# Five edits to an image network's kernel: RNN input kept in SBUF with its statistics, a scale and shift by ScalarE, PSUM copies by ScalarE, two sets of convolution banks, and B's diagonals built two quarters at a time

## Chip, cores and metric

The kernel runs on one core of a Trainium2 chip, all in fp32. The metric is the device time of one execution in microseconds (us). Engines are named as the profile names them: PE (TensorE, with PEld for its weight loads), DVE (VectorE), ACT (ScalarE), POOL (GpSimd) and SP (SyncE, which issues the DMAs here). A `q` behind an engine's name is its sequencer.

## The reference

Two layers over an image batch x of shape (4, 64, 64, 128): 4 images, 4096 tokens each, 128 channels.

```python
x = x + L0_conv(ln(x))        # attention, 4 heads of 32, q and k scaled to norm 1 over tokens
t = tokens(x)
t = t + L0_ffn(ln(t))         # an RNN over 4096 tokens
x = x + L1_conv(ln(x))        # projection, 3x3 convolution, selective scan, projection
t = tokens(x)
t = t + L1_ffn(ln(t))         # 64 experts, 8 tokens each
```

The parts that the change touches:

```python
# L0_ffn
Wx = t @ W.T
Wx = (Wx - mean) * rsqrt(var + 1e-5) * gamma + beta     # over all tokens of all images
y[t] = sigmoid(Wx[t] + y[t-1] @ V.T)
# L1_conv, d = 256 inner channels, N = 16 states, K = 4 directions
xin, z = split(x @ in_proj.T)
u = silu(conv3x3_depthwise(xin) + conv_b)
dt, B, C = projections of u, per direction
h = h * exp(dt * A) + (dt * u) * B                      # per token, 256 x 16 states
y = sum over n of h * C;  + D * u;  directions summed
y = (y - mean) * rsqrt(var + 1e-5) * norm_g + norm_b    # over the 256 channels
out = (y * silu(z)) @ out_proj.T
```

## The kernel before

Channels lie on the 128 partitions and tokens along the free axis. A chunk is 512 tokens (CH), 8 to an image (NCH). The stages are functions called one after another: `attention`, `rnn`, `selective_scan` (its inputs, the scans, its outputs) and `experts`. Between them the activations x1, wx, x2, x3 lie in DRAM. Each stage opens its own pools of SBUF and PSUM. Instructions go to each engine's queue in a planned order, and an engine works its queue off in that order.

**Norms (L85 to L148).** Every layer norm over channels runs in groups of four chunks. `centre` takes the mean by a matmul (L115), subtracts it on DVE (L117), squares on ACT (L118), and sums the squares by a matmul (L121). `end` makes the reciprocal root for an image; `scale` spreads it over the partitions by a matmul (L145) and multiplies on DVE (L148). Setting up its constants costs a few DVE copies (L100).

**Attention.** `attention_of_small` makes q, k and v per chunk: three groups of four matmuls, where v's result goes from a single PSUM bank `v_ps` to SBUF by a DVE copy (L243). Then the long attend loop writes x1. After it the block with pools `af_w` and `af_p` makes the RNN's input: per image it loads x1 again (`x_wx`), runs Norms, multiplies by `w_ffn` (L484), copies PSUM to SBUF by ACT (L486) and writes `wx` to DRAM (L487). The image ahead is centred before the present one is scaled. Behind it stands a branch, `tc.If(flag > 0)` (L176 and L177), for inputs on which the quick form of the softmax doesn't hold; it isn't taken with this data, but all engines meet there. `attention_of_any` holds the other path with its own `wx` code.

**RNN.** `rnn` loads `v_ffn` and `bn`, then each image's `wx` into one large SBUF tile `z` (L697), with a `bn_stats` on DVE for each of 32 chunks (L699), then `bn_aggr` (L701) and small operations on one column, which give gamma and beta folded into a scale and a shift. They are applied to z image by image (L710). After that come the sweeps of the recurrence.

**Scan inputs.** Per image: norm, projection to xin and z, then `convolved` (from L898). The convolution of one half (h) of the 256 channels is done in two groups of four chunks, c0 = 0 and 4. A group is 288 small matmuls (32x32 diagonal weights, L913) into the 4 banks of one PSUM tile `conv_ps` with `bufs=1`, then 16 ACT operations with Silu (L923) that empty it. When a half is whole, POOL makes a copy turned by columns (`uc`, L931), and both go to DRAM. The last image has nothing after it in this stage. The PSUM tags are: `conv` 4 banks, `mm` 3 and `norm` 1.

**Scans.** A schedule written out by hand (`tc.manual_schedule`) runs 144 windows of 16 tiles, one tile a turn. In each turn PE fills `db` (dt u B, L1226), DVE copies a carry into it (L1257) and scans (L1264), ACT makes decays (L1202), and POOL multiplies by C (L1288); PE sums the products (L1317). A generator, `project`, makes the next window's inputs in steps spread over the turns. B's diagonals `b_diag` (L1148) are part of it: B of one quarter of a window (128 partitions x 16 states) times a 32x32 identity, read from PSUM `b_ps`, 128x512 results. Four quarters a window are done one at a time in three turns: one in the turn of `turned(0)`, two in that of `turned(1)`, one more in the next. Half of them, swapped across partitions, go to `b_other` by DMA (L1159 and on).

**Scan outputs.** Per image, ahead by one: y from the directions is summed (L1455) and normed in two halves of channels; per chunk a DVE `tensor_scalar` for each half applies norm_g and norm_b (L1481), DVE multiplies by silu(z) loaded as `z_back` (L1485), PE projects (L1488), DVE adds x2 loaded as `x_back` (L1493), and the sum goes to x3 (L1494). `x_back` and `z_back` have two buffers.

Of the kernel before, what the change touches and what calls it, by code (L numbers as in the profile page):

```python
# [26 lines left out]
P = 128  # L27
# [135 lines left out]
@with_exitstack  # L163
def attention(ctx, tc, a, x1, wx):

    nc = tc.nc
    flag = ctx.enter_context(tc.tile_pool(name="at_f", bufs=1)).tile(
        [1, 1], mybir.dt.int32, name="flag"
    )
    with ExitStack() as inner:
        attention_of_small(inner, tc, a, x1, wx, flag)  # L176
    with tc.If(nc.values_load(flag) > 0):  # L177
        attention_of_any(tc, a, x1, wx)


def attention_of_small(ctx, tc, a, x1, wx, flag):

# [10 lines left out]
    eps6 = constant(nc, cst, 1e-6, "eps6")  # L193
    eps5 = constant(nc, cst, 1e-5, "eps5")
    norms = Norms(nc, cst, ident, C)
# [4 lines left out]
    bo = loaded(nc, cst, a["bo"], "bo")  # L200
    w_ffn = loaded(nc, cst, a["w_ffn"], "w_ffn")
    same_head = constant(nc, cst, 0.0, "same_head", (P, P))
# [18 lines left out]
    def prepare(b, ln_b, r, big, work, ps):  # L221
# [6 lines left out]
        for c in range(NCH):  # L228
            ln = ln_b[:, chunk(c)]
            if c % 4 == 0:  # L230
                norms.scale(ps, r, c // 4, [[ln_b[:, chunk(c + g)]] for g in range(4)])
            for n, (t, w) in enumerate(((q, wq), (k, wk))):
                pt = ps.tile([P, CH], F32, tag="qk", name="qk_ps")
                nc.tensor.matmul(pt, w, ln, start=True, stop=True)
                nc.vector.tensor_copy(t[:, chunk(c)], pt)
                square = work.tile([P, CH], F32, tag="ln_s", name="qk_square")
                nc.scalar.activation(
                    square, t[:, chunk(c)], AF.Square, accum_out=sums[:, n, c : c + 1]
                )
            pt = ps.tile([P, 4, P], F32, tag="v", name="v_ps", bufs=1)  # L240
            for j in range(4):
                nc.tensor.matmul(pt[:, j, :], ln[:, tokens(j)], wv, start=True, stop=True)
            nc.vector.tensor_copy(v[:, 4 * c : 4 * c + 4, :], pt)  # L243
        norm = work.tile([P, 4, 2], F32, tag="norm", name="norm")
# [188 lines left out]
    with (  # L433
# [23 lines left out]
        attend(stream(), work, ps)  # L457
    with (
        tc.tile_pool(name="af_w", bufs=3) as work,
        tc.tile_pool(name="af_p", bufs=2, space=PSUM) as ps,  # L460
    ):
        def centred(b):
            ln = work.tile([P, L], F32, tag="ln_o", name="ln_o")
            var = norms.begin(ps, 2)
            for n in range(NCH // 4):
                xs = []
                for c in range(4 * n, 4 * n + 4):
                    x = work.tile([P, CH], F32, tag="x", name="x_wx", bufs=8)
                    nc.sync.dma_start(x, x1[b][:, chunk(c)])
                    xs.append([x])  # L470
                norms.centre(ps, work, var, n, xs, [[ln[:, chunk(4 * n + g)]] for g in range(4)])
            return ln, norms.end(work, var, eps5)

        ahead = centred(0)
        for b in range(B):
            ln_b, r = ahead
            if b + 1 < B:
                ahead = centred(b + 1)
            for c in range(NCH):
                ln = ln_b[:, chunk(c)]  # L480
                if c % 4 == 0:
                    norms.scale(ps, r, c // 4, [[ln_b[:, chunk(c + g)]] for g in range(4)])
                pt = ps.tile([P, CH], F32, tag="wx", name="wx_ps")
                nc.tensor.matmul(pt, w_ffn, ln, start=True, stop=True)  # L484
                t = work.tile([P, CH], F32, tag="wx_o", name="wx_o")
                nc.scalar.copy(t, pt)  # L486
                nc.sync.dma_start(wx[b][:, chunk(c)], t)  # L487


@with_exitstack  # L490
def attention_of_any(ctx, tc, a, x1, wx):

# [10 lines left out]
    eps6 = constant(nc, cst, 1e-6, "eps6")  # L503
    eps5 = constant(nc, cst, 1e-5, "eps5")
    wq = loaded(nc, cst, a["wq_each"], "wq")
# [3 lines left out]
    bo = loaded(nc, cst, a["bo"], "bo")  # L509
    w_ffn = loaded(nc, cst, a["w_ffn"], "w_ffn")  # L510
    NJ = L // P
# [133 lines left out]
    def finish(b, x):  # L645
        nc.sync.dma_start(x1[b], x)
        for c in range(NCH):
            ln = work.tile([P, CH], F32, tag="ln_o", name="ln_o", bufs=1)
            layer_norm(nc, ps, work, mean_of, [x[:, chunk(c)]], [ln], eps5)
            pt = ps.tile([P, CH], F32, tag="mm", name="wx_ps")  # L650
            nc.tensor.matmul(pt, w_ffn, ln, start=True, stop=True)
            t = work.tile([P, CH], F32, tag="wx_o", name="wx_o", bufs=1)
            nc.scalar.copy(t, pt)
            nc.sync.dma_start(wx[b][:, chunk(c)], t)

# [16 lines left out]
@with_exitstack  # L672
def rnn(ctx, tc, a, x1, wx, x2):

# [6 lines left out]
    cst = ctx.enter_context(tc.tile_pool(name="rn_c", bufs=1))  # L681
    work = ctx.enter_context(tc.tile_pool(name="rn_w", bufs=2))

    ident = cst.tile([P, P], F32, name="ident")
# [5 lines left out]

    z = cst.tile([P, B, L], F32, name="z")

    y = cst.tile([P, B, L + 1], F32, name="y")
    nc.vector.memset(y[:, :, 0:1], 0.0)
    stats = cst.tile([P, B * NCH, nc.vector.BN_STATS_DIM], F32, name="stats")
    for b in range(B):
        nc.sync.dma_start(z[:, b, :], wx[b])  # L697
        for c in range(NCH):
            nc.vector.bn_stats(stats[:, b * NCH + c, :], z[:, b, chunk(c)])  # L699
    mv = cst.tile([P, nc.vector.BN_AGGR_DIM], F32, name="mv")  # L700
# [61 lines left out]
    with tc.If(nc.values_load(flag) > 0):  # L762
        one_by_one(tc, ident, vt, z, y, x1, x2)


# [67 lines left out]
def scan_inputs(ctx, tc, a, x2, us, gates):  # L833
# [65 lines left out]
    def convolved(b):  # L899
        for h in range(ND):  # L900
            u = big.tile([P, L], F32, tag="u", name=f"u_{b}", bufs=2)
            image = xins[b][:, h, :].rearrange("p (h w) -> p h w", w=HW)
            for c0 in range(0, NCH, 4):
                pt = ps.tile([P, 4, CH], F32, tag="conv", name="conv_ps", bufs=1)
                for n, (dy, dx) in enumerate(taps):
                    left, right = max(0, -dx), min(HW, HW - dx)
                    for i in range(4):
                        first = (c0 + i) * RPC
                        top, end = max(first, -dy), min(first + RPC, HW - dy)
                        for r in range(4):  # L910
                            rows = slice(32 * r, 32 * r + 32)
                            to = pt[32 * i : 32 * i + 32, r, :].rearrange("p (h w) -> p h w", w=HW)
                            nc.tensor.matmul(  # L913
                                to[:, top - first : end - first, left:right],
                                diag[rows, h, 3 * (dy + 1) + dx + 1, :],
                                image[rows, top + dy : end + dy, left + dx : right + dx],
                                start=n == 0,
                                stop=n == len(taps) - 1,
                            )
                for r in range(4):  # L920
                    for i in range(4):
                        rows = slice(32 * i, 32 * i + 32)
                        nc.scalar.activation(  # L923
                            u[32 * r : 32 * r + 32, chunk(c0 + i)],
                            pt[rows, r, :],
                            AF.Silu,
                            bias=b_conv[rows, h, r : r + 1],
                        )
# [31 lines left out]
def scans(ctx, tc, a, us, ys):  # L960
# [104 lines left out]
    def project(v):  # L1065
# [80 lines left out]

        def diagonal(i):
            nc.vector.tensor_mul(  # L1148
                v.b_diag[:, i],
                b_ps[:, i].rearrange("p (n o) -> p n o", o=1).to_broadcast([P, N, 32]),  # L1150
                ident32.rearrange("p (o t) -> p o t", o=1).to_broadcast([P, N, 32]),
            )
# [8 lines left out]
        pt = turned(0)  # L1161
        diagonal(0)
        yield 1
        nc.scalar.copy(v.dtu[:, 0], pt)
        yield 1
        pt = turned(1)
        diagonal(1)
        diagonal(2)
        yield 1
        nc.scalar.copy(v.dtu[:, 1], pt)  # L1170
        diagonal(3)
        v.b_other = work.tile([P, NS, N, 32], F32, tag="b_other", name="b_other")
# [256 lines left out]
def scan_outputs(ctx, tc, a, x2, ys, gates, x3):  # L1429
# [38 lines left out]
    for b in range(B):  # L1468
# [3 lines left out]
        for c in range(NCH):  # L1472
# [7 lines left out]
            for h in range(ND):  # L1480
                nc.vector.tensor_scalar(  # L1481
                    t[:, h, :], t[:, h, :], norm[:, 0, h : h + 1], norm[:, 1, h : h + 1],
                    ALU.mult, ALU.add,
                )
# [209 lines left out]
def model(tc, a, out):  # L1694
    with tc.tile_pool(name="between", bufs=1, space=DRAM) as pool:
# [5 lines left out]

        x1, wx, x2, x3 = (images(name) for name in ("x1", "wx", "x2", "x3"))
        attention(tc, a, x1, wx)
        rnn(tc, a, x1, wx, x2)
        selective_scan(tc, a, x2, x3)
# [89 lines left out]
```

## Time and profile before

Three executions took 10324.86, 10325.43 and 10332.41 us; the median is 10325.43.

| what | value |
|---|---|
| profiled execution, its own time | 10315.29 us |
| its span in the profile | 10313.4 us |
| busy PE, DVE, ACT, POOL | 90%, 86%, 66%, 54% |
| scan of DVE (L1264), 2304 | 4763.3 us, 2067 ns each |
| products of POOL (L1288), 2304 | 4506.1 us, 1971 ns each |
| B's diagonals (L1148), 576 | median 683 ns each |
| v copies (L243), 32 | median 692 ns each |
| scale and shift (L1481), 64 | median 542 ns each |
| input statistics (L699), 32 | median 677 ns each |

| stage | from, to (us) |
|---|---|
| q, k and v | 0, 222 |
| attend | 235, 2674 |
| RNN input (wx) | 2676.7, 2786.9 |
| its load, statistics and scale | 2791.3, 2831.5 |
| RNN sweeps, scan inputs | to 3656.7 |
| scans | 3663, 9626 |
| scan outputs | 9631, 9926 |
| experts | 9927, 10313 |

Busy shares are means over stages with different limits, so a stage has to be read by itself. A line number in a row is that of the code; a group's row gives its busy time and the mean of one instruction. "idle 3.1 <-DMA z" is time in which the engine had nothing to do until that transfer came.

### The profile page before, as it was taken

What the parts mean: (1) busy time and instruction counts of PE and PEld (TensorE: products, weight loads), DVE (VectorE), ACT (ScalarE), POOL (GpSimd) and SP (SyncE); (2) the same over time, 40 slices, a digit from 0 to 9 for tenths busy, and PEclk for the clock granted to TensorE, in tenths of its full rate; (3) what the DMA queues carried; (4) which work ended last, traced back from release to release, by engine and by line L of the source; (5) the groups of instructions that cost most, each with busy time, mean ns of one, the idle gap of its engine ahead of it and who ended that gap; (6) DMA issues with size and microseconds to landing.
All of it is one profiled execution on the core that took longest, in us unless ns stands there. A gap on an engine that the chain in (4) does not pass through costs nothing.

```text
span 10313.4 us, 244132 instructions
## 1 busy us (share of the span) xinstructions
PE 9300.8 (90%) x103920; PEld 4392.6 (43%) x103920; DVE 8853.2 (86%) x8023; ACT 6815.1 (66%) x9682; POOL 5613.4 (54%) x3513
## 2 busy tenths in 40 slices
PE   7999999999798779999999999999999999999766
PEld 3222222222233345555555555555555555555323
DVE  7999999999684169999999999999999999999864
ACT  3888888888464557777677777767777776777211
POOL 0000000000011169999999999999999999999200
PEclk8999999999899889999999999999999999999987
DMA  4000000000213245566555566655555555566634
GB/s 182 7 7 32 9 32 9 7 9 7 106 49 110 109 126 143 139 154 158 150 140 147 141 150 154 156 139 139 150 154 150 149 146 136 146 154 156 203 128 168
DMA packets 529251, 1173.63 MB, mean 114 GB/s; under 512 B 47955, under 2 KB 436635, under 8 KB 498331
## 3 DMA queue, kind: packets, MB, share of 16 engines
q1 hardware_dynamic: 528154, 1157.87, 40.3%
q8 instruction: 828, 13.57, 0.5%
q14 instruction: 269, 2.20, 0.1%
HBM read 816.74 MB, written 190.00 MB: 98 GB/s over the span
## 4 chain that ended last, share of the span: by engine, by line
DVE 50%; issue 8%; PE 3%; DMA 2%; DVEq 1%; POOL 0%; ACT 0%; SPq 0%; POOLq 0%; ACTq 0%
DVE states L1264 42%; DVE db L1257 3%; DVE b_diag L1148 1%; DVE log L1120 1%; PE db L1226 0%; DVE y L1455 0%; DVEq L1264 0%; DVEq L1257 0%; PE pool_ps L1575 0%; PE y L1317 0%; PE norm_mean_ps L115 0%; PE gate_ps L1545 0%; DMA weights<-in_w 0%; PE norm_var L121 0%; POOL products L1288 0%
## 5 line engine op out<-in xcount | busy, mean ns | idle before, releaser
L1264 DVE TENSOR_TENSOR_SCAN states<-decays,db 128x920 f32<-128x920 f32 x2304 | 4763.3, 2067 | 175.8 <-DVE db L1257 4.9
L1288 POOL TENSOR_TENSOR products<-states,c_ring 128x912 f32<-128x912 f32 x2304 | 4506.1, 1971 | 431.5 <-DVE db L1257 168.0
L1202 ACT ACTIVATE decays<-dt,a_logs 128x456 f32<-128x456 f32 x4608 | 3100.2, 676 | 97.6
L1226 PEld LDWEIGHTS db<-b_diag,dtu_t 32*128 32x128 f32 x18432 | 2229.3, 187 | 1792.3 <-issue 1332.9
L1226 PE MATMUL db<-b_diag,dtu_t 32*128 32x128 f32 x18432 | 2631.1, 281 | 375.4 <-DVE states L1264 313.6
L1226 PE MATMUL db<-b_other,dtu_t 32*128 32x128 f32 x18432 | 2669.8, 284 | 5.5 <-DMA b_other<-b_diag 3.2
L1235 PE MATMUL y<-zeros 32*128 32x128 f32 x17224 | 2490.7, 283 | 5.0 <-issue 5.0
L1317 PE MATMUL y<-products,ident 64*64 64x456 f32 x18432 | 2309.3, 569 | 6.7 <-issue 4.1
L1226 PEld LDWEIGHTS db<-b_other,dtu_t 32*128 32x128 f32 x18432 | 2231.7, 187 | 6.2 <-DMA b_other<-b_diag 3.8
L1235 PEld LDWEIGHTS y<-zeros 32*128 32x128 f32 x17224 | 2080.5, 186 | 5.0 <-issue 4.8
L333 DVE TENSOR_TENSOR total<-total,ring 128x2048 f32<-128x2048 f32 x768 | 1759.3, 2291 | 65.9 <-DVE total L333 2.8
masks.py:197 POOL MEMSET ident<- 128x128 f32 x6 | 1.2, 204 | 3103.5 <-SPq L177 2789.6
L301 ACT ACTIVATE ring<-sa 128x2048 f32<-128x2048 f32 x640 | 1203.9, 1881 | 452.0 <-PE sa L286 452.0
L1275 ACT COPY carry<-states 128x8 f32<-128x8 f32 x576 | 117.7, 204 | 1668.0 <-DVE states L1264 1621.7
L310 PE MATMUL av<-ring,v_at 128*32 128x512 f32 x8192 | 1010.0, 599 | 0.1
L286 PE MATMUL sa<-q_at,k_at 32*128 32x512 f32 x5120 | 731.8, 641 | 60.9 <-ACT ring L301 35.4
L301 ACT ACTIVATE ring<-sb 128x1536 f32<-128x1536 f32 x512 | 741.3, 1448 | 0.0
L1317 PEld LDWEIGHTS y<-products,ident 64*64 64x64 f32 x18432 | 492.2, 131 | 332.0 <-issue 52.7
L286 PE MATMUL sb<-q_at,k_at 32*128 32x512 f32 x3072 | 555.3, 615 | 50.7 <-ACT ring L301 50.7
L310 PEld LDWEIGHTS av<-ring,v_at 128*32 128x32 f32 x8192 | 210.4, 109 | 700.9 <-issue 676.3
L1257 DVE COPY db<-states 128x8 f32<-128x8 f32 x1728 | 303.1, 175 | 195.0 <-PE db L1226 13.4
L286 PEld LDWEIGHTS sa<-q_at,k_at 32*128 32x128 f32 x5120 | 200.4, 183 | 616.4 <-ACT ring L301 309.7
(208 smaller groups left out, 9162.8 us busy)
## 6 DMA issues: line engine op xcount, KB each, us to landing
c_ring<-c_rows SPq DMA_DIRECT2D x576, 912.0 KB, 7.5
b_other<-b_diag SPq DMA_DIRECT2D x288, 512.0 KB, 9.6
u<-u_r SPq DMA_DIRECT2D x72, 456.0 KB, 10.0
y_r<-sum SPq DMA_DIRECT2D x72, 456.0 KB, 4.2
u<-u_c SPq DMA_DIRECT2D x72, 456.0 KB, 10.1
y_c<-sum SPq DMA_DIRECT2D x72, 456.0 KB, 4.6
weights<-in_w SPq DMA_DIRECT2D x32, 1024.0 KB, 11.9
x<-x SPq DMA_DIRECT2D x96, 256.0 KB, 2.7
```

The source lines that it names most:

```text
L286: nc.tensor.matmul(s[:, m, :], k[rows, tokens(t)], q[rows, chunk(chunk_state["c"])], start=True, stop=True,)
L301: nc.scalar.activation(ring[:, lo : lo + n, :], s[:, at : at + n, :], AF.Exp)
L310: nc.tensor.matmul(chunk_state["av"][rows, :], chunk_state["v"][:, t, rows], ring[:, at + i, :], start=t == 0, stop=t == NJ - 1,)
L333: nc.vector.tensor_add(total, total, w)
L1202: nc.scalar.activation(to, dt, AF.Exp, scale=scale)
L1226: nc.tensor.matmul(bank.rearrange("p (n t) -> p n t", n=4)[:, :, at : at + 32], v.dtu[rows, h, s, :], b[rows, s, 4 * self.q : 4 * self.q + ...
L1235: nc.tensor.matmul(y[:, idle // 2, :P], zeros[rows], zeros[rows], start=False, stop=False)
L1257: nc.vector.tensor_copy(self.edge(self.db[:, SKIP:], v.into), self.edge(before.slot(states), v.outof) if self.nth else self.carry(),)
L1264: nc.vector.tensor_tensor_scan(order(self.slot(states)), order(self.slot(decays, 1 if self.v.back else 0)), order(self.db[:, SKIP:][:, : 2 ...
L1275: nc.scalar.copy(self.carry(), self.edge(self.slot(states), self.v.outof))
L1288: nc.gpsimd.tensor_mul(to, h, c)
L1317: nc.tensor.matmul(to, ident[rows, rows], of, start=begins, stop=ends)
```

## The change

There are five edits.

1. `wx` in DRAM is gone. The block that made it leaves `attention_of_small` and becomes `rnn_inputs`, called in `rnn` after the branch. ACT copies each chunk from PSUM straight into `z`, and the chunk's `bn_stats` is issued right behind the copy. Norms are set up once more there, and `w_ffn` is loaded there. The buffers of the centred image go from 3 to 2. `attention_of_any` loses its `wx` code as well. The tile `y` is made after the block.
2. The v copies are made by ACT instead of DVE.
3. In the last image's convolution the groups c0 = 4 use three banks of `mm` and the one of `norm` instead of `conv`.
4. B's diagonals are made two quarters at a time: `diagonals(0)` in the turn of the first, `diagonals(2)` in that of the second and third; nothing is left in the next turn.
5. Scale and shift in the scan's outputs are ACT operations (Identity with a column of scales and one of biases) instead of DVE ones.

```diff
@@ attention_of_small
-            nc.vector.tensor_copy(v[:, 4 * c : 4 * c + 4, :], pt)
+            nc.scalar.copy(v[:, 4 * c : 4 * c + 4, :], pt)
...
-    with (
-        tc.tile_pool(name="af_w", bufs=3) as work,
-        tc.tile_pool(name="af_p", bufs=2, space=PSUM) as ps,
-    ):
...
-                pt = ps.tile([P, CH], F32, tag="wx", name="wx_ps")
-                nc.tensor.matmul(pt, w_ffn, ln, start=True, stop=True)
-                t = work.tile([P, CH], F32, tag="wx_o", name="wx_o")
-                nc.scalar.copy(t, pt)
-                nc.sync.dma_start(wx[b][:, chunk(c)], t)
@@ rnn
     z = cst.tile([P, B, L], F32, name="z")
+    stats = cst.tile([P, B * NCH, nc.vector.BN_STATS_DIM], F32, name="stats")
+    with ExitStack() as inner:
+        rnn_inputs(inner, tc, a, x1, ident, eps5, z, stats)
...
-    for b in range(B):
-        nc.sync.dma_start(z[:, b, :], wx[b])
-        for c in range(NCH):
-            nc.vector.bn_stats(stats[:, b * NCH + c, :], z[:, b, chunk(c)])
@@ new
+def rnn_inputs(ctx, tc, a, x1, ident, eps5, z, stats):
+    nc = tc.nc
+    cst = ctx.enter_context(tc.tile_pool(name="ri_c", bufs=1))
+    work = ctx.enter_context(tc.tile_pool(name="ri_w", bufs=2))
+    ps = ctx.enter_context(tc.tile_pool(name="ri_p", bufs=2, space=PSUM))
+    norms = Norms(nc, cst, ident, C)
+    w_ffn = loaded(nc, cst, a["w_ffn"], "w_ffn")
...
+    ahead = centred(0)
+    for b in range(B):
+        ln, r = ahead
+        if b + 1 < B:
+            ahead = centred(b + 1)
+        for c in range(NCH):
+            if c % 4 == 0:
+                norms.scale(ps, r, c // 4, [[ln[:, chunk(c + g)]] for g in range(4)])
+            pt = ps.tile([P, CH], F32, tag="wx", name="wx_ps")
+            nc.tensor.matmul(pt, w_ffn, ln[:, chunk(c)], start=True, stop=True)
+            nc.scalar.copy(z[:, b, chunk(c)], pt)
+            nc.vector.bn_stats(stats[:, b * NCH + c, :], z[:, b, chunk(c)])
@@ convolved
-                pt = ps.tile([P, 4, CH], F32, tag="conv", name="conv_ps", bufs=1)
+                if b == B - 1 and c0:
+                    pt = [ps.tile([P, CH], F32, tag="mm", name="conv_ps") for _ in range(3)]
+                    pt.append(ps.tile([P, CH], F32, tag="norm", name="conv_ps", bufs=1))
+                else:
+                    pt = ps.tile([P, 4, CH], F32, tag="conv", name="conv_ps", bufs=1)
+                    pt = [pt[:, r, :] for r in range(4)]
@@ project
-        def diagonal(i):
+        def diagonals(i):
             nc.vector.tensor_mul(
-                v.b_diag[:, i],
-                b_ps[:, i].rearrange("p (n o) -> p n o", o=1).to_broadcast([P, N, 32]),
-                ident32.rearrange("p (o t) -> p o t", o=1).to_broadcast([P, N, 32]),
+                v.b_diag[:, i : i + 2].rearrange("p s n t -> p (s n) t"),
+                b_ps[:, i : i + 2]
+                .rearrange("p s (n o) -> p (s n) o", o=1)
+                .to_broadcast([P, 2 * N, 32]),
+                ident32.rearrange("p (o t) -> p o t", o=1).to_broadcast([P, 2 * N, 32]),
             )
...
         pt = turned(0)
-        diagonal(0)
+        diagonals(0)
...
         pt = turned(1)
-        diagonal(1)
-        diagonal(2)
+        diagonals(2)
         yield 1
         nc.scalar.copy(v.dtu[:, 1], pt)
-        diagonal(3)
@@ scan_outputs
             for h in range(ND):
-                nc.vector.tensor_scalar(
-                    t[:, h, :], t[:, h, :], norm[:, 0, h : h + 1], norm[:, 1, h : h + 1],
-                    ALU.mult, ALU.add,
-                )
+                nc.scalar.activation(
+                    t[:, h, :],
+                    t[:, h, :],
+                    AF.Identity,
+                    scale=norm[:, 0, h : h + 1],
+                    bias=norm[:, 1, h : h + 1],
+                )
```

## The prediction

> **What bounds the kernel now.** I read the page's chain of waits first, then the timeline around the convolution, then the one around the RNN's input, then the busy time by stretches, then VectorE (DVE) alone inside the scan. The profiled execution took 10315.29 us (span 10313.4, 1.9 around it), 10.1 less than the median 10325.43; I sum against the execution and carry the sum over to the median.
>
> The chain, by engine and by line:
>
> ```profile
> DVE 50%; issue 8%; PE 3%; DMA 2%; DVEq 1%; POOL 0%; ACT 0%; SPq 0%; POOLq 0%; ACTq 0%
> DVE states L1264 42%; DVE db L1257 3%; DVE b_diag L1148 1%; DVE log L1120 1%; PE db L1226 0%; DVE y L1455 0%; DVEq L1264 0%; DVEq L1257 0%; PE pool_ps L1575 0%; PE y L1317 0%; PE norm_mean_ps L115 0%; PE gate_ps L1545 0%; DMA weights<-in_w 0%; PE norm_var L121 0%; POOL products L1288 0%
> ```
>
> The scan's VectorE work ends last, and B's diagonals (L1148) stand on it. The stages follow one another behind barriers, so a stage that ends earlier moves everything after it. The last image's convolution (columns: start, duration, engine, line, what; in brackets the idle time before):
>
> ```profile
> 3558.00 10.71 PE L913 MATMUL conv_ps<-xin,diag 32*32 32x512 f32 x286
> 3568.79 11.06 ACT L923 ACTIVATE u<-conv_ps,b_conv 32x512 f32<-32x512 f32 x16 [10.09 <-PE conv_ps L913]
> 3579.91 11.56 PE L913 MATMUL conv_ps<-xin,diag 32*32 32x512 f32 x288 [11.20 <-ACT u L923]
> 3591.57 11.06 ACT L923 ACTIVATE u<-conv_ps,b_conv 32x512 f32<-32x512 f32 x16 [11.72 <-PE conv_ps L913]
> ...
> 3638.43 11.06 ACT L923 ACTIVATE u<-conv_ps,b_conv 32x512 f32<-32x512 f32 x16 [12.44 <-PE conv_ps L913]
> ...
> 3649.61 7.06 POOL L931 COPY uc<-u 128x4096 f32<-128x4096 f32 x1 [39.47 <-ACT u L923]
> ```
>
> TensorE and ScalarE take turns, each idle while the other works, and the stage's last copy waits for the eighth turn. The seam between attention and the RNN:
>
> ```profile
> 2786.01 0.59 ACT L486 COPY wx_o<-wx_ps 128x512 f32<-128x512 f32 x1 [0.28 <-PE wx_ps L484]
> ...
> 2791.28 0.34 SPq L159 DMA_DIRECT2D v_ffn<-in_v_ffn  x1
> ...
> 2792.14 2.13 SPq L697 DMA_DIRECT2D z<-wx  x4
> ...
> 2800.28 19.56 DVE L699 BATCH_NORM_STATS2 stats<-z 128x6 f32<-128x512 f32 x32 [6.32 <-DMA z<-wx]
> 2819.87 1.02 DVE L701 BATCH_NORM_AGGREGATE mv<-stats 128x2 f32<-128x192 f32 x1
> ```
>
> After the last copy come a barrier, a load, and 32 statistics alone on the path. Stretches (start:end, length, then busy PE, PEld, DVE, ACT, POOL, granted clock, DMA share):
>
> ```profile
> 2676.00:2791.00 115.00, 100.42 (x256) 30.70 (x256) 54.65 (x71) 42.67 (x69) 0.11 (x1) 0.93 0.42 148
> 9719.00:9784.00 65.00, 50.56 (x112) 16.25 (x112) 59.63 (x82) 10.27 (x17) 0.00 (x0) 0.89 0.76 250
> 9848.00:9926.00 78.00, 52.72 (x84) 18.32 (x84) 60.83 (x93) 0.00 (x0) 0.00 (x0) 0.76 0.60 192
> ```
>
> In the first TensorE is full and VectorE half idle; in the others, from the scan's output stage, VectorE is nearly full.
>
> **RNN input in SBUF.** From the end of the last L486 copy (2786.60) to the aggregate (2819.87) are 33.3 us: all of it goes except a last statistic behind its copy. The 32 statistics (0.677 each, 0.61 apart) move into the 115 us where VectorE is busy 55; they stand in its queue behind ScalarE's copies, and the next image's centring and L148 products queue behind them, and TensorE's next matmuls for those. Laying them by hand between the rows costs under 1 us per image, mostly caught up, 0.4 at the end. The 32 writes of 256 KB (L487) and 4 loads of z leave SP's queue. But the barrier of the branch now stands ahead of this stage: last x1 write issued until 2674.94, plus the 4.34 that the barrier takes at the seam (last wx issue ends 2786.94, first issue after it 2791.28) is 2679.3; three small weight issues (0.34 to 0.45 each) make the first x load 2680.5 instead of 2676.72: 3.8 later. The new Norms constants (VectorE 1.8 us) hide under that load's 5.4. Aggregate at 2786.6+3.8+0.4+1.0 = 2791.8: **−28** (−32 if the barrier is short; −24 if the statistics hold up the products by 1 us an image).
>
> **v copies to ScalarE.** 32 copies of 0.69 leave VectorE, 32 of some 0.59 (L486's form) join ScalarE, which is busy about 2.2 of each chunk's 2.6 us with them. TensorE paces the chunks (three groups of 0.86), so both are hidden; the v bank is released 0.2 to 0.4 us ahead of its next use. VectorE's 13.5 us at image ends no longer hold v: **−1** (−7, if all of TensorE's waits for L243, 4.3 us, and its followers go, to +4 if the slack is short by 0.12 in each of 32 chunks).
>
> **Two sets of banks.** TensorE's second group no longer waits for ScalarE. Its four groups run at 10.7, 11.6, 12.2, 12.3 from 3558.0 to 3604.8; ScalarE's fourth turn ends 11.1 later, 3616, instead of 3649.5: **−34** (−37 if ScalarE's 4 × 11.06 from 3568.79 bind, −30 if each hand-over costs 1 us). The image's other half is copied by POOL (7.4) before that. 0 if the sets don't overlap.
>
> **Diagonals in pairs.** 576 of 128x512 become 288 of 128x1024. VectorE in one window of 16 scans:
>
> ```profile
> 6016.55 2.07 DVE L1264 TENSOR_TENSOR_SCAN states<-decays,db 128x920 f32<-128x920 f32 x1
> ...
> 6018.59 0.69 DVE L1148 TENSOR_TENSOR b_diag<-b_ps,ident 128x512 f32<-128x512 f32 x1
> 6019.19 2.06 DVE L1264 TENSOR_TENSOR_SCAN states<-decays,db 128x920 f32<-128x920 f32 x1
> ...
> 6021.63 2.07 DVE L1264 TENSOR_TENSOR_SCAN states<-decays,db 128x920 f32<-128x920 f32 x1
> ...
> 6023.88 1.28 DVE L1148 TENSOR_TENSOR b_diag<-b_ps,ident 128x512 f32<-128x512 f32 x2
> 6025.08 2.06 DVE L1264 TENSOR_TENSOR_SCAN states<-decays,db 128x920 f32<-128x920 f32 x1
> ```
>
> A plain turn of scan to scan is 2.45 us (2.275 where the carry is copied in), of which VectorE is idle some 0.3. Over all windows the turn with one diagonal is longer by 0.366, the one with two by 1.002, the third (one) by 0.363: 1.731 a window. So the first diagonal of a turn hides half of itself in the idle time, and the second pays 0.636. The change makes two turns with one 1024 and a third with none. The 1024 is 0.683 plus what 512 more elements cost: 1.221 − 0.686 = 0.535 by L1485 (128x1024 against 128x512). So 2 × (0.366 to 0.40 + 0.535) = 1.80 to 1.87 against 1.731: the instructions saved had been hidden in part. 144 windows × 0.08: **+12** (+21 at most by this; −42 if busy time counted, 576 × 0.683 − 288 × 1.22).
>
> The Trainium skill, "Perfetto Trace Analysis", section Optimizing Scalar/DVE Operations, gives VectorE an overhead of about 125 ns an instruction on PSUM and advises larger operations if the engine is saturated. By that, an estimate, 288 instructions fewer would gain 36 us where I book 12 of loss; the idle 0.3 in each turn says that the engine isn't saturated in its sense.
>
> **Scale and shift by ScalarE.** 64 tensor_scalar of 0.542, 0.455 apart, leave VectorE: 29.1 us; ScalarE gets 64 of about 0.63 (L118, 128x512 from SBUF; 0.70 by L365, with a bias), 40 to 45 us, and is idle 233 of the stage's 275. Images 0 and 1: VectorE 59.6 of 65, so 16 × 0.455 = 7.3 comes off, less a hand-over: 6 each. The last two (78 us, 32 of these operations, 14.6 on VectorE) also wait for out_ps and for the two slots of x_back, some 3.6 a chunk against today's 4.7: 9. Together **−21** (−29 to −8, the latter if each added hop between engines is exposed in the tail).
>
> The skill's "ScalarE: Activation LUTs", section Rules for kernel authors, says add and mul belong on VectorE. Its section What ACT_TABLE_LOAD costs would make one of these 0.80 us (an estimate: 186 + 0.833 × 512 ns and two pointer operands of 93), 51 in all; still below ScalarE's idle time, so the sum would stay.
>
> **Sum.** −28 − 1 − 34 + 12 − 21 = −72: 10243.3 for an execution like the profiled one, **10253** against the median.
>
> **Rivals.** (A) The pairs gain. For: VectorE is the chain. Against: the idle time in each turn. By the 0.064 that two single operations take over one wide one (1.28 − 1.216), 288 × 0.064 = −18; by busy rows −42: 10223 to 10199. (B) The hops eat the gains: every edit but the pairs at its small end, −24 + 4 − 30 + 12 − 8 = −46, 10279; or the two bank sets wait for one another, 10253 + 34 = 10287. For: both are new waits between engines; against: nothing else asks for those banks at the end. (C) Slower: a 1024-wide product with two broadcast operands runs below one element a cycle, or delays the scan and with it POOL's products. The rest gains 84; it decides from 84/144 = 0.58 us a window over today's 1.73, and at half rate (2 × 1.07 more) it costs 307 + 12: 10560. For: POOL and VectorE are both over 0.9 busy there. Against: the 512-wide one takes 0.683, no more than a plain product (0.686).
>
> **How the numbers follow.** Forecast 0.64 (own range 10235 to 10272), A 0.17, B 0.13, C 0.06. A difference below 0.2% (20.7 us) can't be told from none. Faster: the first three but a remnant, 0.90; same 0.04 (C near its threshold, or B with a dearer pair); slower 0.06. The range takes in the better half of A and all of B's sums but the bank sets at naught.
>
> **What would show it.** The aggregate near 2792, with x loads from 2680; ScalarE's four L923 groups one behind another, POOL's last uc near 3616 less 28; scan turns of about 3.35, 3.17 and 2.45 where today there are 3.45, 2.64 and 2.85, a 1024-wide product near 1.22; the output stage near 255 us instead of 275. I am wrong if the scan stage changes by over 0.15 us a window or ScalarE's hops show as VectorE's idle time in the output stage.

## The result and the profile after

The changed kernel takes 10247.51 us (median of 4 runs, 10237.57 to 10252.78) against 10326.43 us before (median of 4, 10324.86 to 10332.41). The ratio is 0.9921, 95% interval 0.9904 to 0.9939. A later comparison gave 0.9917 (0.9904 to 0.9931). The profiled execution took 10249.59 us, its span is 10247.8 us, and that is 65.6 less than the span before. The medians differ by 78.9, because the profiled execution before lay 11 us under its median and the one after 2 over. Stage by stage, the two traces and the forecast compare like this (us):

| stretch | before | after | measured | forecast |
|---|---|---|---|---|
| start to first attend matmul | 235.0 | 232.4 | -2.6 | -1 (v copies) |
| to the last write of x1 | 2439.7 | 2441.0 | +1.3 | 0 |
| to the aggregate of the RNN's statistics | 145.2 | 117.7 | -27.5 | -28 |
| to the last image's last `uc` copy | 829.7 | 794.1 | -35.6 | -34 |
| to the first scan | 56.8 | 54.4 | -2.4 | 0 |
| first to last scan | 5915.5 | 5939.9 | +24.4 | +12 |
| to the experts' first load | 305.4 | 284.9 | -20.5 | -21 |
| to the end | 386.0 | 383.4 | -2.6 | 0 |

The chain of waits after, by engine and line:

```profile
DVE 49%; issue 9%; PE 4%; DMA 2%; DVEq 1%; POOL 0%; ACT 0%; SPq 0%; POOLq 0%; ACTq 0%
DVE states L1261 43%; DVE db L1254 4%; DVE log L1116 1%; DMA weights<-in_w 1%; DVEq L1261 1%; PE db L1223 0%; PE norm_mean_ps L115 0%; DMA x_back<-x 0%; PE y L1314 0%; PE scatter_ps L1683 0%; DVEq L1254 0%; DMA y<-y_r 0%; DVE y L1452 0%; PE gate_ps L1545 0%; PE norm_each L145 0%
```

The scans on DVE still end last. The diagonals have dropped out of the listed lines, but that isn't their price, as the experiments show. The seam before the RNN, on the timeline after (start, duration, engine, line, what):

```profile
2673.40 0.32 SPq L368 DMA_DIRECT2D x<-x_at  x1
...
2676.92 0.33 SPq L159 DMA_DIRECT2D v_ffn<-in_v_ffn  x1
...
2678.24 55.28 SPq L737 DMA_DIRECT2D x_wx<-x  x32
...
2789.76 0.58 ACT L752 COPY z<-wx_ps 128x512 f32<-128x512 f32 x1 [0.27 <-PE wx_ps L751]
...
2790.38 0.69 DVE L753 BATCH_NORM_STATS2 stats<-z 128x6 f32<-128x512 f32 x1
...
2791.11 1.02 DVE L656 BATCH_NORM_AGGREGATE mv<-stats 128x2 f32<-128x192 f32 x1
```

The barrier now shows between the last write and the first load (3.2 us), and only one statistic and the aggregate follow the last copy: from its start to the aggregate's, 1.3 us where 33.9 had been. From the first weight load for x_wx to the start of the last copy it is 107.8 us instead of 106.0. The stage is 1.7 to 1.8 longer; that the statistics among the other DVE work are the reason isn't shown, because the buffers of the centred image went from 3 to 2 as well, and a later run with the old way (wx through DRAM, below) took 106.8 for this piece.

The last image's convolution, on the same timeline:

```profile
3538.46 11.04 PE L909 MATMUL conv_ps<-xin,diag 32*32 32x512 f32 x321 [1.75 <-issue]
3540.83 44.29 ACT L919 ACTIVATE u<-conv_ps,b_conv 32x512 f32<-32x512 f32 x64 [11.01 <-PE conv_ps L909]
3551.93 10.09 PE L909 MATMUL conv_ps<-xin,diag 32*32 32x512 f32 x294 [2.43 <-ACT u L919]
...
3585.24 7.05 POOL L927 COPY uc<-u 128x4096 f32<-128x4096 f32 x1 [14.57 <-ACT u L919]
```

The 64 ACT operations of the four groups are one unbroken piece of 44.29 us. Before, they stretched over 80.7 us (3568.79 to 3649.49).

### The profile page after: what moved, and what is told of

It is laid out like the page before. It is cut to its first block, busy times and chain, and to the rows that moved or that the text cites. A ratio compares the mean times of both kernels' runs of the same rounds, so it can differ in the third digit from the quotient of the medians.

```text
span 10247.8 us, 243786 instructions
## 1 busy us (share of the span) xinstructions
PE 9262.8 (90%) x103920; PEld 4423.3 (43%) x103920; DVE 8805.9 (86%) x7650; ACT 6876.9 (67%) x9778; POOL 5617.5 (55%) x3513
## 4 chain that ended last, share of the span: by engine, by line
DVE 49%; issue 9%; PE 4%; DMA 2%; DVEq 1%; POOL 0%; ACT 0%; SPq 0%; POOLq 0%; ACTq 0%
DVE states L1261 43%; DVE db L1254 4%; DVE log L1116 1%; DMA weights<-in_w 1%; DVEq L1261 1%; PE db L1223 0%; PE norm_mean_ps L115 0%; DMA x_back<-x 0%; PE y L1314 0%; PE scatter_ps L1683 0%; DVEq L1254 0%; DMA y<-y_r 0%; DVE y L1452 0%; PE gate_ps L1545 0%; PE norm_each L145 0%
## 5 line engine op out<-in xcount | busy, mean ns | idle before, releaser
L1232 PE MATMUL y<-zeros 32*128 32x128 f32 x17224 | 2515.9, 284 | 0.6 <-issue 0.5
```

What stands on the lines that cost most here:

```text
L1232: nc.tensor.matmul(y[:, idle // 2, :P], zeros[rows], zeros[rows], start=False, stop=False)
```

## The experiments

In the stage times below "scan stage" means first to last scan as in the table; the expectations count to the last scan's end, 2 us more. The changed kernel's own scatter shows in a second run of it, and in others whose scans are the same code: 5939.9, 5937.8, 5930.2, 5934.2, 5930.5, 5934.7 us.

**The base again.**

> The changed kernel once more, beside the kernel before, as the base for the next three. Its scan stage, first to last scan, was 5942 us against 5918 before; of these 24, the turns that hold diagonals explain 14 (+0.53, -0.06, -0.37 us a window), and 10 lie spread over turns whose work is the same. If the 10 belong to the change, the stage is 5942 +- 2 again and the plain turns are again some 0.006 us longer than before; if they are scatter between executions, they come out elsewhere by several us. Kernel 10247, ratio 0.992.

10244.87 us against 10327.65; scan stage 5937.8. To part the work from chance, take the median over 144 windows at each of the 16 turns, and sum. That gives 5891.6 us before and 5906.3 after, 5904.9 here (for all 2304 turns; the stage has one fewer); all that turns took beyond these medians is 26.5 before, 36.1 after and 35.5 here. In four further runs with the same pairs it was 26.2 to 31.0 (the sum of medians 5905.7 to 5906.9). So the pairs cost 14 us, and the other 10 are scatter between executions, of which the one before was a low draw.

**Four quarters again.** The edit restores the old function and its calls:

```diff
...
-        diagonals(0)
+        diagonal(0)
...
-        diagonals(2)
+        diagonal(1)
+        diagonal(2)
         yield 1
         nc.scalar.copy(v.dtu[:, 1], pt)
+        diagonal(3)
```

> The changed kernel with B's diagonals one quarter at a time as before (four 512-wide in turns 3, 5, 5, 6). Theory (the first operation of a turn hides half of itself in the idle time between two scans, what comes on top pays in full): turns of 2.64, 3.45, 2.85 again, 1.73 us a window instead of 1.84, the scan stage 14 us shorter, or 24 if the rest was caused by the pairs too; kernel 10223 to 10234, ratio about 0.990. Rival (fewer, larger operations are cheaper): the stage gets 18 to 42 us longer, kernel 10265 to 10290.

Scan stage 5924.2, 13.6 less than in the base beside it; turns 2.64, 3.45 and 2.85 again. The kernel took 10241.44 (ratio 0.9914, 0.9901 to 0.9928): 3.4 under the base by medians, which can't be told from none. The rival's 18 to 42 us the other way are out. The turns of the changed kernel show why. This is its DVE timeline in one window:

```profile
6004.42 2.07 DVE L1261 TENSOR_TENSOR_SCAN states<-decays,db 128x920 f32<-128x920 f32 x1
...
6006.46 1.22 DVE L1145 TENSOR_TENSOR b_diag<-b_ps,ident 128x1024 f32<-128x1024 f32 x1
6007.60 2.06 DVE L1261 TENSOR_TENSOR_SCAN states<-decays,db 128x920 f32<-128x920 f32 x1
...
6010.03 2.07 DVE L1261 TENSOR_TENSOR_SCAN states<-decays,db 128x920 f32<-128x920 f32 x1
...
6012.29 1.21 DVE L1145 TENSOR_TENSOR b_diag<-b_ps,ident 128x1024 f32<-128x1024 f32 x1
6013.42 2.06 DVE L1261 TENSOR_TENSOR_SCAN states<-decays,db 128x920 f32<-128x920 f32 x1
6015.89 2.07 DVE L1261 TENSOR_TENSOR_SCAN states<-decays,db 128x920 f32<-128x920 f32 x1
```

Scan to scan, the first pair makes 6004.42 to 6007.60, 3.18; the second 3.39; the turn behind has none and takes 2.47. Beyond plain turns that is 0.90 + 0.94 = 1.84 a window against 1.73 in quarters. Of the 0.68 us of work taken out of the third turn (2.85 before), only 0.37 came off its length; the rest became idle time there.

**One a turn.** The four quarters again, but the second goes to the turn between (shown against the run with four quarters):

```diff
         nc.scalar.copy(v.dtu[:, 0], pt)
+        diagonal(1)
         yield 1
         pt = turned(1)
-        diagonal(1)
         diagonal(2)
```

> The changed kernel with four 512-wide diagonals, one in each of four turns (3, 4, 5, 6), so that none is second in its turn. Theory: each costs about 0.37 us, 1.47 a window instead of 1.84, the scan stage some 52 us shorter than in the changed kernel, near 5888 us; kernel about 10195, ratio 0.987. Rival (VectorE's busy time is what counts): the same 576 operations as with quarters in three turns, so the same time as that one to within 3 us.

10212.69 us, ratio 0.9886 (0.9871 to 0.9901), apart from the base's interval in the same comparison; scan stage 5899.2, that is 38.6 less than the base and 25.0 less than with the same 576 instructions in three turns. DVE's timeline of this kernel:

```profile
5993.49 2.06 DVE L1260 TENSOR_TENSOR_SCAN states<-decays,db 128x920 f32<-128x920 f32 x1
5995.65 0.18 DVE L1253 COPY db<-states 128x8 f32<-128x8 f32 x1
5995.73 0.68 DVE L1144 TENSOR_TENSOR b_diag<-b_ps,ident 128x512 f32<-128x512 f32 x1
5996.33 2.06 DVE L1260 TENSOR_TENSOR_SCAN states<-decays,db 128x920 f32<-128x920 f32 x1
```

By medians over the windows, three of the four turns take 2.84 with the 0.68 us operation and the one where the carry is copied in takes 2.64. That is only 0.36 to 0.41 beyond plain ones; four cost 1.53, a little over the 1.47 expected, and the gain of 38.6 is short of the 52 expected. Busy time as the measure is ruled out: this kernel has DVE's busy work of the quarters and is faster.

**All in one.** One operation of 128x2048 in turn 3, `diagonals(2)` removed.

```diff
-                v.b_diag[:, i : i + 2].rearrange("p s n t -> p (s n) t"),
-                b_ps[:, i : i + 2]
+                v.b_diag[:, i : i + 4].rearrange("p s n t -> p (s n) t"),
+                b_ps[:, i : i + 4]
...
```

> The changed kernel with all four quarters in one 128x2048 operation in turn 3. Theory: it takes 2.28 us busy and makes that turn 2.275 + 0.366 + 3 x 0.535 = 4.25, 1.97 us a window instead of 1.84: 19 us more, kernel about 10266, unless POOL or ScalarE use the long turn to get ahead. Rival (fewer, larger operations are cheaper): 144 operations fewer at 0.06 to 0.14 us each, 9 to 20 us less, kernel about 10232.

10386.25 us, slower than the kernel before (1.0051, 1.0037 to 1.0064). The turn itself was as worked out, 4.24 us, and both theories missed the rest: in 54 of 143 windows turn 6 (turns are counted from 0) takes over 3 us (median 2.48). The busy time by stretches around one such place (start:end, length, busy PE, PEld, DVE, ACT, POOL, then PE's granted clock as a share of full speed, the DMA share and GB/s):

```profile
5996.00:5999.00 3.00, 1.06 (x12) 0.30 (x15) 2.84 (x3) 2.91 (x6) 3.00 (x4) 1.00 0.00 0
...
6001.50:6005.00 3.50, 3.50 (x40) 2.82 (x42) 2.29 (x3) 2.54 (x4) 3.28 (x2) 0.68 0.40 135
```

PE is idle for 1.94 us behind the long turn, and then its clock reads 0.68, a mean over that stretch; the transposes of dt u (L1140) take 1.97 us instead of 1.09, the next fill is late, and DVE waits for it. On the timelines of PE and DVE:

```profile
6001.29 1.97 PE L1140 MATMUL dtu_ps<-ident,e_dtu 128*64 128x128 f32 x16
...
6004.64 0.17 DVE L1253 COPY db<-states 128x8 f32<-128x8 f32 x1 [1.07 <-PE db L1222]
```

Every window has about that idle time, but in only 49 of 143 do the transposes take over 1.3 us (1 of 143 in the changed kernel, whose idle time there is 0.9; that one stands at the start of the stage in every kernel here).

The trace also says which windows these are. All 218 changes of the granted clock that it records lie on one grid with a step of 3.41 us (to within 0.01 us), and the clock is either 1.0 or 0.5. These are two pairs of neighbouring steps, from the window above and the next one, where PE's idle time begins later in its step:

```profile
5996.91:6000.32 3.41, 1.51 (x28) 1.21 (x32) 3.20 (x3) 3.03 (x6) 3.41 (x4) 1.00 0.00 0
6000.32:6003.73 3.41, 3.41 (x28) 2.11 (x22) 3.04 (x3) 2.29 (x4) 3.19 (x3) 0.50 0.06 17
...
6037.87:6041.28 3.41, 1.93 (x32) 1.02 (x32) 3.41 (x2) 3.29 (x7) 3.41 (x4) 1.00 0.02 6
6041.28:6044.69 3.41, 2.95 (x48) 2.07 (x48) 3.00 (x5) 2.40 (x5) 3.41 (x3) 1.00 0.03 5
```

With 1.90 us of idle time in one step the clock is 0.50 in the next; with 1.48 in one step and the rest in the next it stays. Over all windows: where at least 1.55 us fell into one step (a bound fitted to these windows), the clock fell behind 52 of 56; behind the other 87 it fell once. This sorts the windows of one trace; no run moved the idle time against the grid on purpose.

**Keeping PE at work.** Three kernels add matmuls of zeros into the running sum behind the long turn. First 18 on one strip of 32 rows:

```diff
         nc.scalar.copy(v.dtu[:, 0], pt)
+        if summed[-1] is not None:
+            for _ in range(18):
+                rows = slice(32, 64)
+                nc.tensor.matmul(
+                    summed[-1][:, 0, :P], zeros[rows], zeros[rows], start=False, stop=False
+                )
         yield 1
```

> All four diagonals in one 128x2048 operation, as in the run that took 10386 us, with 18 more matmuls of zeros into the running sum in the turn behind, where TensorE was idle for 1.9 us and its granted clock fell to 0.68. The edit adds 2592 such matmuls and nothing else. Theory (the long turn leaves TensorE idle, its clock falls, and the transposes and fills behind it come late to VectorE): TensorE stays at its clock, turns 6 to 8 are 2.48, 2.27 and 2.45 again, and the scan stage falls from 6070 to 5955 to 5965, kernel near 10266 to 10275. Rival (the turns behind are late because ScalarE, POOL or the transfer of the other half of the diagonals is late): the stage stays within 15 us of 6070, or grows by the added matmuls.

10930.24 us: neither theory. The 18 took 4.3 us, over twice the time meant for them, and the clock fell all the same: the transposes are slow in 119 of 143 windows. On PE's timeline, and by stretches:

```profile
6005.62 3.94 PE L1167 MATMUL y<-zeros 32*128 32x128 f32 x33
```

```profile
6010.70:6012.50 1.80, 1.80 (x9) 0.30 (x8) 1.70 (x2) 0.00 (x0) 1.49 (x1) 0.50 0.00 0
```

The first row holds 33 of the 36 records of the 18; the others follow among the next fill's. PE had been busy without a break from 6003 on, 7.7 us, at a clock of 0.97 or more, and then it is 0.50. By the same steps, it fell behind all but 4 of the 135 windows with at least 2.4 us of the added matmuls in one step, and behind none of the 7 with less (again a fitted bound). Then 8 pairs on two strips, sized to the idle time:

```diff
+            for i in range(8):
+                for strip in (1, 2):
+                    rows = slice(32 * strip, 32 * strip + 32)
+                    nc.tensor.matmul(
+                        summed[-1][:, strip // 2, :P],
...
```

> The 128x2048 diagonals again, with 16 matmuls of zeros behind the long turn, on two strips of the array at once, so that they take some 1.75 us of TensorE's 1.9 us of idle time (the 18 on one strip took 3.9 us, ran past it and made the next fill late). They add nothing to the sum. Theory (in a third of the windows TensorE's clock falls after that idle time, which makes the transposes take 1.97 us instead of 1.09 and the fills late): no fall, the transposes take 1.09 in nearly all windows, the scan stage is 5955 to 5970 instead of 6070, kernel near 10270. Rival (the fall comes whatever TensorE does there, as with the 18): the stage stays over 6040.

10280.15 us, scan stage 5962.8: as the theory had it, 107 of the 132 us that the wide operation had cost over the base are back with matmuls that compute nothing. Slow transposes only in the 1 window at the start. The stretch behind a long turn:

```profile
5977.40:5979.80 2.40, 2.40 (x43) 1.92 (x38) 2.21 (x3) 2.32 (x6) 2.40 (x3) 1.00 0.00 0
```

And 8 on one strip, the same loop as the 18 but shorter:

```diff
-            for _ in range(18):
+            for _ in range(8):
```

> The 128x2048 diagonals with 8 matmuls of zeros on one strip behind the long turn, where the last such run had 8 pairs on two strips: the same 1.75 us of TensorE, half the array in use at a time. It parts the two things that differed between the 18 on one strip (transposes slow in 119 of 143 windows) and the 8 pairs on two (slow in 1). If TensorE only has to be busy, and the 18 failed by running past the idle time: slow in a few windows, scan stage near 5963 us, kernel near 10275. If the width in use counts: slow in at least a third of the windows again, stage at 6040 or more, kernel above 10350.

Between the two: 10306.09 us, scan stage 5994.7, slow transposes in 14 windows, against 49 with nothing and 1 with two strips. But for the one at the start, all are among the 44 windows where one step of the grid held all of the added matmuls; in the 98 where a step ended among them, the clock never fell there. So most of the fall came from PE being idle, and part of it from how little of the array is in use. How the chip weighs the two within a step isn't settled by this.

**The other parts undone, one at a time.** Scale and shift on DVE:

```diff
-                nc.scalar.activation(
-                    t[:, h, :],
-                    t[:, h, :],
-                    AF.Identity,
-                    scale=norm[:, 0, h : h + 1],
-                    bias=norm[:, 1, h : h + 1],
+                nc.vector.tensor_scalar(
+                    t[:, h, :], t[:, h, :], norm[:, 0, h : h + 1], norm[:, 1, h : h + 1],
+                    ALU.mult, ALU.add,
                 )
```

> The changed kernel with the scale and shift of the scan's outputs on VectorE again. Theory: VectorE bounds that stage, so from the last scan to the experts' first load it takes some 304 us again instead of 283 to 288: +18 to +21, kernel near 10266. Rival (the stage is bound by its loads and stores, and the gain came from elsewhere): under +6. Beside it, the scan stage tells of the 10 us that lie outside the turns with diagonals: if this edit caused them, they are gone here (stage near 5930); if they are scatter of the one profiled execution of the kernel before, the stage is 5938 to 5942 as in the changed kernel.

10266.98 us; from the last scan to the experts' load 306.0 against 283.6 to 288.2 in the kernels with the edit: 18 to 22 us, as expected. The scan stage is 5930.2, which by the expectation would put the spare 10 us on this edit. But the sum of medians is the same (5905.7), and the runs below that keep the edit have 5930.5 to 5934.7: scatter, not this edit.

One set of banks:

```diff
-                if b == B - 1 and c0:
+                if False:
```

> The changed kernel with one set of convolution banks for the last image as before. Theory: TensorE and ScalarE take turns again and the last image's four groups take 81 us from the first ScalarE turn instead of 44: +36, kernel near 10282. Rival (TensorE, or its clock after idle time, limits the four groups anyway): under +20. Scan stage as in the changed kernel if the spare 10 us are scatter.

10285.37 us. From the start of the first of the last image's 64 ACT operations to the end of the last it is 80.25 us, against 44.3 to 44.6 in the kernels with two sets: 35.7 to 36.0. (The longer stretch from the aggregate to the last `uc` scatters between 784.5 and 804.4 in kernels of the same code there, and was 832.7 here.) The rival's bound of 20 is passed.

The RNN's input through DRAM (the kernel before with the other four edits), at its core:

```diff
-            nc.scalar.copy(z[:, b, chunk(c)], pt)
-            nc.vector.bn_stats(stats[:, b * NCH + c, :], z[:, b, chunk(c)])
+                t = work.tile([P, CH], F32, tag="wx_o", name="wx_o")
+                nc.scalar.copy(t, pt)
+                nc.sync.dma_start(wx[b][:, chunk(c)], t)
```

> The changed kernel without its first edit: the RNN's input goes through DRAM again, with the statistics behind the load; the other four edits stay. Theory: from the last write of x1 to the aggregate 145 us again instead of 118: +27 to +28, kernel near 10273. Rival (the statistics hold up the next image's products, and the copies are held up by them, so that most of the gain is given back): under +20.

10274.5 us; from the last x1 write to the aggregate 146.0 instead of 117.7, so 28.3. The rival, that the statistics give back most of it, is out.

v copies on DVE:

```diff
-            nc.scalar.copy(v[:, 4 * c : 4 * c + 4, :], pt)
+            nc.vector.tensor_copy(v[:, 4 * c : 4 * c + 4, :], pt)
```

> The changed kernel with the v copies on VectorE again. Theory (hidden behind TensorE but for the ends of images): the first attend matmul comes at 233 to 235 us instead of 231 to 233, kernel +1 to +2. Rival (ScalarE's copies hold up its squares and the v bank): attend starts earlier than 231.

10244.77 us, not to be told from the base. The first attend matmul came at 234.6 us, against 230.7 to 233.3 in the traces with the copies on ACT: 1 to 4 us, the size expected, but no more than an indication.

**A better version tried.** One diagonal a turn, and four buffers for x_back:

```diff
-            x = work.tile([P, CH], F32, tag="x", name="x_back")
+            x = work.tile([P, CH], F32, tag="x", name="x_back", bufs=4)
```

> One diagonal a turn in four turns, as in the run that took 10213 us, and four buffers instead of two for x_back in the scan's outputs. Theory (the tail of that stage waits for the two slots: a store and a load in sequence, some 3.6 us a chunk): from the last scan to the experts' first load 283 to 288 us fall by 6 to 15, kernel 10198 to 10207. Rival (the tail is set by the sums, z_back or the two out_ps banks): within 3 us of before, kernel 10213 plus or minus 4.

10210.23 us, ratio 0.9888 (0.9871 to 0.9904). From the last scan to the experts' load 283.3, 4.5 less than in the run with one diagonal a turn and two buffers, but others with two buffers had 283.6. Under the 6 us expected, with the whole time where the rival had it, and inconclusive: the ring isn't shown to bound that tail.

## Why the prediction was right, step by step

The forecast was 10253 and the median 10247.51; the sum of the terms -72 against -65.6 between the two traces and -78.9 between the medians. So it lies between two measures that differ by the scatter of single executions, and a hit to 6 us is partly luck: in the traces the scans' 12 us over the forecast are about half made up for by small gains that it had at nothing or too low (-2.4 before the first scan, -2.6 at the end, -1.6 more each before the attend loop and in the scan inputs).

- **RNN input, -28; -27.5.** The barrier was shorter than forecast (v_ffn issued 3.2 us after the write instead of 4.34, the first x load at 2678.2 instead of 2680.5, of which 1.2 come from the last write's being earlier), and the stage longer (1.7 to 1.8 instead of 0.4), and these nearly cancel. Undoing it cost 28.3.
- **v copies, -1.** 2.6 by one pair of traces; the undo could not separate it from zero in the whole.
- **Two bank sets, -34; -35.6.** ScalarE's four groups bound, without gaps, 44.3 us where there had been 80.7: 36.4 less. The sum had TensorE's groups bind and this only as its better end (-37); so the mechanism was the forecast's side case, and some 2 us the difference. That the longer stretch in the table came out so near is luck, since it scatters by 20 us in kernels of the same code. Rival B's worst case, sets that wait for one another, is refuted by the unbroken row. Undoing it gave the time back.
- **Diagonals, +12; +14 by medians of turns.** The turns came out at 3.39, 3.18 and 2.47 where 3.35, 3.17 and 2.45 had been forecast. The 1024-wide operation took 1.217, as expected (1.216). Rival A (busy time or instruction count) is refuted by the quarters, and more clearly by the four in four turns. Rival C's slow broadcast did not occur. But its other half, that a long turn makes others late, exists for one step wider: 128x2048 tips it, through PE's clock, a way that the prediction had not considered.
- **Scale and shift, -21; -20.5.** The operation took longer than the prediction's rows for it, 0.80 instead of 0.63 to 0.70 (L1478 below), without a sign that this cost anything: ScalarE is busy for 91 of the stage's 285 us. The Trainium skill's page "ScalarE: Activation LUTs", section What ACT_TABLE_LOAD costs, which adds about 93 ns for each pointer operand, gave 0.80 as well, by the prediction's estimate from it: here the page was nearer than the rows. By images, each counted up to its last store, the first gained 5.6, the second 5.2 and the last two 9.6, where 6, 6 and 9 had been forecast.

By groups, in the changed kernel's output stage, and what DVE waits for there (waiter, what it waits for: us, times, longest):

```profile
L1478 ACT ACTIVATE ln_y<-ln_y,norm 128x512 f32<-128x512 f32 x64 | 48.1, 805 | 48.4 <-DVE ln_y L148 48.4
```

```profile
DVE x_back L1493 <- DMA x_back<-x: 12.4, 12, 4.0
DVE x_back L1493 <- PE out_ps L1488: 10.9, 8, 2.4
...
DVE ln_y L1485 <- ACT ln_y L1478: 0.9, 1, 0.9
```

DVE itself waits for the new hop between engines once, for 0.9 us. What it waits for now is x_back and the projection. From the last scan to the experts' first load DVE is busy 214.1 us instead of 242.6 and idle 70.8 instead of 62.8: 28.5 of work went, and 8 of it came back as idle time. The sum had allowed for as much (29.1 of work for 21 of gain). TensorE's weight loads wait for the new operation 8 times, 13.8 us in all.

The Trainium skill's page "Perfetto Trace Analysis", section Optimizing Scalar/DVE Operations, says that larger operations can improve throughput if the engine is saturated. These runs show DVE 0.93 busy in the scan stage and yet not saturated in that sense, since a turn pays only some 0.37 to 0.4 of the first 0.68 us put into it. Against four quarters in three turns (scan stage 5924.2), merging two cost 14 us, merging four 145, and the same four in four turns gained 25.

## What to carry to other kernels

In a loop whose steps leave the busiest engine a short idle time each, part of an extra operation hides in that time once a step, about half of a 0.68 us one here: spread small operations over the steps rather than merge them, and price them by the difference in step length, not by busy time. Where two stages alternate through one set of buffers at the end of a phase, with nothing behind to overlap, any banks free at that point make a second set. Before lengthening a step, look at which engine the longer step leaves idle, and what follows on it.

## What the runs showed of the hardware

In these traces TensorE's granted clock changes only on a grid with a step of 3.41 us, and falls to half. Behind 1.94 us of idle time, transposes took 1.97 us instead of 1.09 in 49 of 143 windows; behind 0.9 us in none but the one at the stage's start, which every kernel here has. What parts the windows is how much of the idle time lies in one step: with 1.55 us or more the clock fell in 52 of 56 windows, with less in 1 of 87. Busy time alone does not hold it: behind 4.3 us of matmuls on one strip of 32 rows the transposes were slow in 119 windows, behind 2.05 us of them in 14, with two strips only in the one at the start. "TensorE: Matmul & The Clock Gate" of the Trainium skill, section HAM oscillation — how this bites in real kernels, gives as the rule no idle gaps over some 3.4 us; here 1.94 were enough in about a third of the windows, so that for this kernel the measurement, not the rule, is the bound.
